# A ternary product fed by two float32r parts of its rows instead of three bfloat16 parts, in a one-core perceiver kernel

## The chip, the cores and the metric

The kernel runs on one core of one Trainium2 chip. The core has five engines with queues of their own: TensorE (PE; its weight loads are listed as PEld), VectorE (DVE), ScalarE (ACT), GpSimd (POOL) and SyncE (SP), which here only issues transfers. The metric is the device time of one execution in microseconds; the figure for a kernel is the median of its runs.

## What is computed

The reference is a two-layer perceiver over 128 independent batches of 32 latent rows (width 256) and 257 context rows each. Cut to its last lines it is

```python
x = x + _L0_xattn_ref(ctx_1024, _layernorm(x), wq, wk, wv)     # softmax attention over the context
x = x + _L0_attn_ref(_layernorm(x), ...)                        # selective scan, 512 channels x 16 states
x = x + _L0_ffn_ref(_layernorm(x), W_fc, ln_w, ln_b, W_proj)    # the feed-forward that the change touches
x = x + _L1_xattn_ref(_layernorm(x), ctx_1024, ctx_1024, ...)   # linear attention with focused feature maps
x = x + _L1_attn_ref(_layernorm(x), ...)                        # latent attention with decay
x = x + _L1_ffn_ref(_layernorm(x), w1, b1, w2, b2)              # quantized feed-forward
```

and the part that matters is

```python
def _L0_ffn_ref(x, W_fc, ln_w, ln_b, W_proj):
    h = jnp.einsum('btd,hd->bth', x, absmean(W_fc))     # absmean: every weight becomes -1, 0 or 1
    h = jax.nn.gelu(h, approximate=False)
    h = layernorm(h, ln_w, ln_b)
    return jnp.einsum('bth,dh->btd', h, absmean(W_proj))
```

The first product has 256 inputs and 1024 hidden units. Its weights are ternary, so they are exact in any type; the precision of the product is that of the rows `x`.

## The kernel before

**Tiling.** Four batches of 32 rows make a group of 128 rows, which fill the 128 partitions; there are 32 groups. Groups are taken in nine blocks of 2, 4, 4, 4, 4, 4, 4, 4 and 2 (`BLOCKS`). For each block the program records, one after the other: for each group the context part (`context_group`: loads, transposes of the context, softmax attention, then keys and values for the linear attention of layer 1, in the tiles `pkey`, `ku`, `ks`, `pval`, `vf` and `pk`); the scan of the whole block (`scan_block`: projections `pproj`, then for each of 4 x 16 channel-state pairs an exponential `a` on ACT, a scan `h` on DVE and a weighted sum on DVE or POOL); and for each group the latent part (`latent_group`: `mlp`, `linear`, `attention`, `quantized_mlp`).

**What sets the order.** Nothing is issued as it is recorded. A `Recorder` collects all operations with their reads, writes and an estimated duration, and `order` (L403) places them like a list scheduler. Every recorded part has a window in the table `DUE`, from which each operation gets a due time; on each engine the operation due soonest goes first among those that could start soon enough (`WINDOW`). `SOONER` favours operations that free PSUM, `AHEAD` pulls transfers forward, `HORIZON` limits how far ahead a new buffer is opened. An operation that may run on several engines (`copy`: ACT or DVE; `cast`: ACT or POOL) goes where its start, plus its duration weighted by `PRICE`, is lowest. The order that comes out is a fixed program order on each engine, and each engine works strictly along it. All these operations are issued from one line, L575, in `trace`; names of tiles tell them apart.

**Buffers.** Tiles come from rings: `t4` (4 buffers of 4 KB per partition), `t2` (17 of 2 KB, `t2k`, L693), `t1` (7 of 1 KB, `t1k`) and eight PSUM banks (`bank`). The plan may open a tile only where the ring has a buffer free. The 2 KB ring serves, among others, the scan's `h`, `dl`, `some` and four `yg` a block, `ku` and `ks` of the keys, and `x3` below.

**Fill products.** Where the plan leaves PE idle for more than 600 ns, `keep_busy` (L553) adds products of constants into the bank that is about to be used, issued from L562:

```python
for _ in range(int(FILL * (op.gap - 200.0) / 216.0)):      # FILL is 0.7
```

They compute nothing that is used.

**The first product of the MLP** (`mlp`, L1223). The rows of a group, less their mean, are transposed by PE into a bank `pT` and copied by ACT to `xT` (f32). Then they are split into three bfloat16 parts in the tile `x3` (the profile shows it as `x`): a cast, a subtraction on POOL of what the cast kept, a second cast, and a second subtraction on POOL that writes the third part. For each half of the 1024 hidden units, six products accumulate in one bank `ph`: two halves of the 256 inputs times three parts, each 128 x 128 x 512 in bfloat16, with the rows as stationary operand and `w_fc` as moving one. ACT applies the gelu, DVE takes statistics, PE transposes `hid`, and the second product `pmlp` runs in plain f32. `w_fc` is made once, in `late_setup`, by the function `ternary`, which writes -1, 0 and 1 straight into a bfloat16 tile (L746) of 4 KB per partition.

**Key-value sums** (`keys_values`, L1121). Each group adds four sums, one a batch, into the bank `pk`; the last one recorded closes the accumulation.

Of the kernel before, what the change touches and what calls it, by code (L numbers as in the profile page):

```python
# [9 lines left out]
BF16 = mybir.dt.bfloat16  # L10
I32 = mybir.dt.int32
AF = mybir.ActivationFunctionType
ALU = mybir.AluOpType
# [3 lines left out]
P = 128  # L17
# [91 lines left out]
def size_of(a):  # L109
    n = 1  # L110
    for k in a.shape[1:]:
        n *= k
    return n
# [153 lines left out]
class Recorder:  # L267
# [62 lines left out]
    def record(self, calls):  # L330
        ways = {}
        for engine, (name, args, kw) in calls.items():
# [25 lines left out]
            ways[engine] = [(name, args, kw)], ns, locks  # L358
        reads = [b for b in map(box_of, ins) if b]
        writes = [b for b in map(box_of, outs) if b]  # L360
        bufs = [a.buf for a in (*ins, *outs) if isinstance(a, View)]
        self.keep += bufs
        self.bufs_of.update((id(b), b) for b in bufs)
        if self.joined is not None:
            small = ins[0].shape[0] < P or size_of(ins[0]) < P
            self.joined.append((*ways["tensor"][:2], reads, writes, small))
            return
        landing = 0
        if "sync" in ways:
            size = size_of(out) * P * 4 if writes else 0  # L370
            landing = 2000 + size / 180.0
        self.add(ways, reads, writes, table, landing)
# [218 lines left out]
PRICE = {"tensor": 0.0, "vector": 28.013093, "scalar": 4.356996, "gpsimd": 3.720234, "sync": 0.0}  # L591
WINDOW = 13.821085
SOONER = 0.0675
AHEAD = 0.744939
HORIZON = 1.665209
# [3 lines left out]
def perceiver_kernel(ctx: ExitStack, tc: tile.TileContext, t: dict, out: bass.AP):  # L599
# [93 lines left out]
    def t2k(shape, name, dtype=F32):  # L693
        return ring("t2", 17).tile(shape, name, dtype)

    def t1k(shape, name, dtype=F32):
        return ring("t1", 7).tile(shape, name, dtype)
# [48 lines left out]
    w_fc = wts.tile([P, 2, HID], BF16, name="w_fc")  # L746
# [246 lines left out]
    def context_group(b0, xg, kvc):  # L993
# [91 lines left out]
        with R.together():  # L1085
            for m in range(8):
                t_ = slice(m % 4 * 32, m % 4 * 32 + 32)
                R.tensor.matmul(
                    pk[t_, m // 4].rearrange("p b k -> p (b k)"),
                    plg[:, m * 32 : (m + 1) * 32],  # L1090
                    vlz[:, m].rearrange("p b k -> p (b k)"),
                    start=m < 4, stop=False,
                )
        for b in range(0, GB, PAIR):
            zs = keys(cTs[b : b + PAIR])
            for i in range(PAIR):
                keys_values(cTs[b + i], zs[i], pk[:, :, b + i, :], b + i == GB - 1)
# [23 lines left out]
    def keys_values(cT, z, pk, last):  # L1121
# [20 lines left out]
        R.gpsimd.tensor_copy(vf[:, :, :, 16], f.unsqueeze(2).to_broadcast([P, 2, NH]))  # L1142
        with R.together():
            for c in range(2):
                for j in range(2):
                    for m in range(4 * c, 4 * c + 4):
# [5 lines left out]
                        )  # L1152

# [69 lines left out]
    def mlp(xg):  # L1223
# [3 lines left out]
        xT = t1k([P, D], "xT")  # L1227
        transposed(xc, xT.rearrange("p (c n) -> p c n", c=2), 2)

        x3 = t2k([P, 3, D], "x3", BF16)  # L1230
        R.cast(x3[:, 0, :], xT)
        R.gpsimd.tensor_tensor(xT, xT, x3[:, 0, :], ALU.subtract)
        R.cast(x3[:, 1, :], xT)
        R.gpsimd.tensor_tensor(x3[:, 2, :], xT, x3[:, 1, :], ALU.subtract)
# [3 lines left out]
        for k in range(2):  # L1238
            ph = bank("ph")
            cols = slice(k * 512, (k + 1) * 512)  # L1240
            with R.together():
                accumulate(ph, [
                    (x3[:, k3, dc * P : (dc + 1) * P], w_fc[:, dc, cols])
                    for dc in range(2) for k3 in range(3)
                ])
# [267 lines left out]
    (-1.233024, -0.335498), (0.019828, 0.480193), (-1.629912, -0.869437), (-0.837897, -0.738361),  # L1513
    (-0.093681, -0.088914), (-0.021839, -0.017211), (0.306149, 0.488484), (0.39917, 0.543159),
    (0.505346, 1.339487), (0.48714, 0.600075), (0.577018, 0.904067), (0.865508, 1.005891),
    (1.046044, 1.425814), (1.390255, 1.643429), (1.317874, 1.43935), (1.798509, 1.951231),
    (2.102721, 2.277249), (2.253363, 2.602763), (2.83034, 2.835295), (1.877067, 1.881711),
    (1.451009, 1.899495), (0.786758, 1.881711), (1.887508, 2.002024), (0.636118, 0.718999),
    (0.728345, 0.76535), (0.753626, 0.774222), (0.721695, 1.041519), (1.02934, 1.176199),
    (1.193086, 1.242338), (1.482066, 1.506436), (1.570038, 1.574756), (1.52572, 1.568128),  # L1520
    (1.582666, 1.870871), (1.996577, 2.069774), (2.143081, 2.422113), (2.358304, 2.65149),
    (2.69793, 2.755759), (2.394754, 2.76594), (2.909432, 3.128141), (3.227729, 3.512565),
    (3.409932, 3.76627), (2.727973, 3.098836), (3.085723, 3.337484), (3.365331, 3.681179),
    (3.656735, 4.119898), (2.875393, 3.198347), (3.111345, 3.33781), (3.418247, 3.706203),
    (3.705912, 4.06225), (3.050509, 3.381501), (3.357332, 3.56083), (3.584301, 3.855628),
    (3.839172, 4.228837), (1.635373, 1.790687), (1.595887, 1.641535), (1.962785, 2.117782),
    (2.053357, 2.161526), (2.195383, 2.199528), (2.205476, 2.209605), (2.389908, 2.395792),
    (2.486901, 2.49243), (2.488439, 2.647508), (2.615044, 2.87897), (2.840922, 3.128108),
    (3.030885, 3.414002), (3.317041, 3.762668), (3.556818, 3.693699), (3.66408, 3.911331),
    (3.779069, 4.169666), (4.40464, 4.40964), (4.420203, 4.76275), (3.72375, 4.048085),  # L1530
    (4.091394, 4.323445), (4.208163, 4.522378), (4.569256, 4.925594), (3.85714, 4.180094),
    (4.257484, 4.482106), (4.435791, 4.690815), (4.424337, 4.851387), (3.983018, 4.55219),
    (4.391584, 4.396584), (4.348461, 4.54678), (4.768461, 5.107725), (2.594693, 2.67371),
    (2.676285, 2.763798), (2.912055, 2.916796), (2.949665, 3.029696), (3.19548, 3.202614),
    (3.201985, 3.267525), (3.370849, 3.437113), (3.357869, 3.499671), (3.422175, 3.546126),
    (3.536298, 3.791633), (3.827101, 4.085596), (4.097429, 4.412778), (4.392392, 4.655498),
    (4.693, 4.866463), (4.036996, 4.310319), (4.858234, 5.11216), (5.047385, 5.382144),
    (5.400897, 5.766052), (4.741086, 5.03528), (5.046704, 5.271326), (5.279494, 5.56433),
    (5.556414, 5.882502), (4.706208, 4.941658), (5.205771, 5.425698), (5.421318, 5.709504),
    (5.507902, 5.512902), (5.023502, 5.345889), (5.321575, 5.568746), (5.570116, 5.854452),  # L1540
    (5.880912, 6.216796), (3.643344, 3.71582), (3.765067, 3.84418), (3.787796, 3.900941),
    (4.065296, 4.070275), (4.162677, 4.239555), (4.077256, 4.22408), (4.388544, 4.42773),
    (4.425818, 4.457414), (4.539487, 4.592008), (4.671053, 4.971619), (4.919167, 5.210754),
    (5.182193, 5.441083), (5.441083, 5.698089), (5.733278, 5.738278), (5.27428, 5.53055),
    (5.897482, 6.1173), (5.879768, 6.449337), (6.407415, 6.764085), (5.692519, 6.052832),
    (6.046377, 6.27138), (5.860084, 6.537213), (6.550022, 6.906966), (5.877385, 6.208316),
    (6.196681, 6.421303), (6.422896, 6.706139), (6.695526, 7.043141), (6.036972, 6.355891),
    (6.270476, 6.526377), (6.57082, 6.856055), (6.792378, 7.195162), (4.655912, 4.660912),
    (4.67689, 4.774904), (4.974338, 4.979338), (5.031969, 5.241355), (5.15376, 5.208739),
    (5.208182, 5.362023), (5.36406, 5.420469), (5.452575, 5.58779), (5.498786, 5.63902),  # L1550
    (5.613721, 5.894373), (5.872873, 6.132026), (6.156801, 6.412601), (6.400357, 6.652506),
    (6.652075, 6.657075), (6.553174, 7.05071), (6.816602, 6.998958), (7.18521, 7.372307),
    (7.415066, 7.753978), (6.720233, 7.046956), (7.022044, 7.269572), (7.354633, 7.359633),
    (7.519057, 7.88096), (6.879083, 7.195618), (7.19559, 7.440215), (7.420282, 7.694224),
    (7.705356, 8.061949), (7.020903, 7.344351), (7.361654, 7.570043), (7.532526, 7.817798),
    (7.900297, 8.217473), (5.571057, 5.60675), (5.694226, 5.774033), (5.850032, 5.910131),
    (5.899092, 5.961479), (6.160411, 6.165411), (6.187877, 6.292569), (6.437907, 6.442483),
    (6.440971, 6.515481), (6.499997, 6.614903), (6.615753, 6.87484), (6.873594, 7.132682),
    (7.131911, 7.39192), (7.391788, 7.650876), (7.652298, 7.698741), (7.687389, 7.904001),
    (7.908329, 8.089699), (7.975111, 8.03271), (8.430878, 8.761522), (7.723787, 7.798595),  # L1560
    (8.152372, 8.33892), (8.301126, 8.415202), (9.120664, 9.680432), (8.269822, 8.363895),
# [92 lines left out]
```

## Time and profile before

| | |
|---|---|
| time, median of 3 runs | 1715.9 us (1712.74, 1715.9, 1718.06) |
| span of the profiled execution, first to last instruction | 1714.2 us (a time of its own is not listed for it; the median lies 1.7 us above its span) |
| PE, PEld busy | 1650.3 us, 1200.9 us |
| DVE, ACT, POOL busy | 1501.8, 1422.8, 1362.6 us |
| chain that ended last, by engine | PE 48%, DVE 24%, ACT 15%, POOL 10% |
| products into `ph` | 384, 91.5 us |
| granted TensorE clock, mean | 0.996 |

The profile was taken by the hardware profiler on one execution. The page gives busy time, share and count for each engine, and then the span in 40 equal slices, in which a digit is the busy share in tenths. In the table of groups a line reads: line, engine, operation, output <- inputs with their shapes, count; then busy time and mean ns of one; then the idle time of that engine just before, and what ended it. Several products in flight overlap, so the busy time of a group is less than count times mean. A product in plain f32 shows as two records. "The chain" follows the last instruction back, step by step, to what released it.

### The profile page before, as it was taken

The page shows a single profiled execution, that of the slowest core. Times are in us where ns is not written, and L with a number is a line of the kernel's source. Part 1 is how long each engine was busy: PE and PEld are TensorE (multiplying, and loading weights), DVE is VectorE, ACT ScalarE, POOL GpSimd, SP SyncE. Part 2 cuts the span into 40 slices and gives each one's busy share as a digit, 9 for nine tenths or more (in the row PEclk, how much of TensorE's full clock was granted, in tenths as well). Part 3 has the DMA queues.
Part 4 walks back from the last instruction along what each step waited for, and adds up shares of the span by engine and source line. Part 5 has one row for each costly group of instructions (what it writes and reads, how often), then busy time and mean ns, then how long its engine had stood idle before and what let it go on. Part 6 is the DMA issues. An engine that isn't in the chain of part 4 may idle for free.

```text
span 1714.2 us, 45797 instructions
## 1 busy us (share of the span) xinstructions
PE 1650.3 (96%) x17587; PEld 1200.9 (70%) x17587; DVE 1501.8 (88%) x2960; ACT 1422.8 (83%) x3484; POOL 1362.6 (79%) x2152
## 2 busy tenths in 40 slices
PE   8999999999999999999999999999999989899986
PEld 6778777767677767766777777777777666666664
DVE  5389699988997997959998997979999899999777
ACT  4587789888988899779888998889998888788676
POOL 6668769768795888688878678886898699788887
PEclk9999999999999999999999999999999999999999
DMA  8312100110010102001100012010110000000000
GB/s 235 99 60 72 30 29 30 57 35 7 29 54 5 35 14 63 30 2 45 38 30 29 8 42 63 3 29 10 61 42 30 2 20 8 4 4 2 5 9 22
DMA packets 44762, 59.74 MB, mean 35 GB/s; under 512 B 8704, under 2 KB 27008, under 8 KB 44544
## 3 DMA queue, kind: packets, MB, share of 16 engines
q1 hardware_dynamic: 44544, 56.81, 10.7%
q8 instruction: 139, 2.28, 0.6%
q14 instruction: 79, 0.65, 0.1%
HBM read 52.32 MB, written 4.19 MB: 33 GB/s over the span
## 4 chain that ended last, share of the span: by engine, by line
PE 48%; DVE 24%; ACT 15%; POOL 10%; issue 3%; DMA 0%; DVEq 0%; POOLq 0%; ACTq 0%; SPq 0%
DVE h L575 10%; PE pkey L575 7%; PE pproj L575 7%; PE pval L575 6%; DVE acc L575 5%; PE pT L575 3%; PE pmlp L575 3%; PE pqa L575 3%; POOL ku L575 3%; ACT a L575 2%; PE pk L575 2%; ACT ks L575 2%; ACT L575 2%; PE pka L575 2%; PE pcT L575 2%
## 5 line engine op out<-in xcount | busy, mean ns | idle before, releaser
L575 DVE TENSOR_TENSOR_SCAN h<-a,pproj 128x512 f32<-128x512 f32 (+1 forms) x576 | 613.9, 1087 | 22.6 <-ACT a L575 12.5
L575 ACT ACTIVATE a<-dl,a_neg 128x496 f32<-128x496 f32 (+1 forms) x576 | 367.5, 664 | 57.7 <-DVE h L575 53.6
L575 DVE SCALAR_TENSOR_TENSOR acc<-h,w_st,acc 128x512 f32<-128x512 f32 (+1 forms) x436 | 299.9, 688 | 0.7
L575 PE MATMUL pval<-wkv,cT 128*128 128x256 f32 x1024 | 243.9, 384 | 0.1
L575 PE MATMUL pkey<-wkv,cT 128*128 128x256 f32 x1024 | 238.1, 386 | 0.0
L575 ACT ACTIVATE ks<-ku 128x256 f32<-128x256 f32 x512 | 209.1, 415 | 19.3 <-POOL ku L575 17.9
L575 PEld LDWEIGHTS pkey<-wkv,cT 128*128 128x128 f32 x1024 | 189.3, 190 | 39.0 <-issue 15.6
L575 PEld LDWEIGHTS pval<-wkv,cT 128*128 128x128 f32 x1024 | 188.0, 190 | 32.0 <-issue 4.5
L575 POOL TENSOR_TENSOR ku<-ku,e 128x512 f32<-128x512 f32 x128 | 162.8, 1280 | 31.3 <-ACT ku L575 30.0
L575 POOL TENSOR_TENSOR ku<-ks,ku 128x512 f32<-128x512 f32 x128 | 164.4, 1290 | 16.9 <-ACT ks L575 15.8
L575 POOL TENSOR_TENSOR kn<-kn,halves 128x4 f32<-128x4 f32 x128 | 134.3, 1052 | 23.5 <-ACT ks L575 21.9
L575 ACT ACTIVATE vf<-pval,kf 128x256 f32<-128x256 f32 x256 | 108.3, 475 | 31.1 <-PE pval L575 26.3
L575 POOL TENSOR_TENSOR rstd<-rstd,halves 128x1 f32<-128x1 f32 x224 | 126.1, 567 | 6.1
L575 PE MATMUL pproj<-xTs,w_in 128*128 128x512 f32 (+1 forms) x288 | 122.8, 554 | 2.2 <-DVE x L575 1.3
L575 ACT ACT_TABLE_LOAD x95 | 121.9, 1283 | 2.3 <-DVE hq L575 0.6
L575 POOL TENSOR_TENSOR some<-some,h 128x512 f32<-128x512 f32 (+1 forms) x104 | 115.2, 1107 | 3.5
L575 PE MATMUL pmlp<-w_pr,hT 128*128 128x256 f32 x512 | 117.3, 383 | 0.6 <-DVE x L575 0.6
L575 PEld LDWEIGHTS pmlp<-w_pr,hT 128*128 128x128 f32 x512 | 96.2, 191 | 14.7 <-DVE x L575 0.7
L575 POOL TENSOR_SCALAR h<-h,w_st 128x512 f32<-128x512 f32 (+1 forms) x104 | 65.3, 629 | 51.0 <-DVE h L575 32.7
L575 ACT ACTIVATION_READ_ACCUMULATOR ks<-ku 128x1 f32 x512 | 100.8, 197 | 0.0
L575 POOL TENSOR_SCALAR rstd<-mv 128x1 f32<-128x1 f32 x224 | 45.4, 203 | 67.5 <-DVE mv L575 43.3
L575 PE MATMUL ph<-w_fc,x 128*128 128x512 bf16 x384 | 91.5, 380 | 0.3 <-ACT vf L575 0.2
(289 smaller groups left out, 3867.0 us busy)
## 6 DMA issues: line engine op xcount, KB each, us to landing
cx<-in_ctx_dram SPq DMA_DIRECT2D x64, 512.0 KB
x<-in_x_dram SPq DMA_DIRECT2D x32, 128.0 KB
cr<-in_ctx_dram SPq DMA_DIRECT2D x128, 32.0 KB
out_dram<-x SPq DMA_DIRECT2D x32, 128.0 KB
vlz<-vl SPq DMA_DIRECT2D x128, 1.1 KB
w_in<-in_w_inT_dram SPq DMA_DIRECT2D x1, 1024.0 KB
raw_fc<-in_w_fcT_dram SPq DMA_DIRECT2D x2, 512.0 KB
raw_pr<-in_w_prT_dram SPq DMA_DIRECT2D x2, 512.0 KB
```

What stands on the lines that cost most here:

```text
L575: ins = getattr(engine, name)(*(traced(a) for a in args), **{k: traced(v) for k, v in kw.items()}).ins
```

## The change

- `w_fc` becomes a tile of type float32r, with four bytes an element, so 8 KB per partition in place of 4.
- `mlp` keeps the transposed rows in the bank `pT` and makes two float32r parts of them, in two 1 KB tiles (both named `xT` and a number): a copy of the bank, on ACT or DVE, and on DVE the bank less that copy. The f32 copy `xT`, the tile `x3`, both casts and both subtractions on POOL go.
- A half of the hidden units is now four products (two halves of the inputs times two parts) in place of six.
- The 2 KB ring has 15 buffers in place of 17.
- `PRICE`, `WINDOW`, `SOONER`, `AHEAD`, `HORIZON` and the whole table `DUE` have new values, so every engine's order is new.
- The recorder's `record` is split in two (`cost` is new) and takes lists of calls; no call hands it one. `keys_values` takes the list of the sums placed before it, and the last sum of a group must follow the other three.

```diff
-PRICE = {"tensor": 0.0, "vector": 28.013093, "scalar": 4.356996, "gpsimd": 3.720234, "sync": 0.0}
-WINDOW = 13.821085
-SOONER = 0.0675
-AHEAD = 0.744939
-HORIZON = 1.665209
+PRICE = {"tensor": 0.0, "vector": 45.207809, "scalar": 8.002797, "gpsimd": 6.895979, "sync": 0.0}
+WINDOW = 13.504066
+SOONER = 0.067879
+AHEAD = 0.971922
+HORIZON = 1.829143
...
-        return ring("t2", 17).tile(shape, name, dtype)
+        return ring("t2", 15).tile(shape, name, dtype)
...
-    w_fc = wts.tile([P, 2, HID], BF16, name="w_fc")
+    w_fc = wts.tile([P, 2, HID], F32R, name="w_fc")
...
+        last = len(sums) == GB - 1
+        R.first = tuple(sums) if last else ()
         with R.together():
...
-        xT = t1k([P, D], "xT")
-        transposed(xc, xT.rearrange("p (c n) -> p c n", c=2), 2)
-
-        x3 = t2k([P, 3, D], "x3", BF16)
-        R.cast(x3[:, 0, :], xT)
-        R.gpsimd.tensor_tensor(xT, xT, x3[:, 0, :], ALU.subtract)
-        R.cast(x3[:, 1, :], xT)
-        R.gpsimd.tensor_tensor(x3[:, 2, :], xT, x3[:, 1, :], ALU.subtract)
+        xs = [t1k([P, D], f"xT{k}", F32R) for k in range(2)]
+        pt = bank("pT")
+        with R.together():
+            for c in range(2):
+                cols = slice(c * P, (c + 1) * P)
+                R.tensor.transpose(pt[:, cols], xc[:, cols], ident)
+        R.copy(xs[0], pt[:, 0:D])
+        R.vector.tensor_tensor(xs[1], pt[:, 0:D], xs[0], ALU.subtract)
...
                 accumulate(ph, [
-                    (x3[:, k3, dc * P : (dc + 1) * P], w_fc[:, dc, cols])
-                    for dc in range(2) for k3 in range(3)
+                    (part[:, dc * P : (dc + 1) * P], w_fc[:, dc, cols])
+                    for dc in range(2) for part in xs
                 ])
```

## The prediction, made before the changed kernel ran

> **What bounds the kernel now.** I read the page's busy shares and slices first.
>
> ```profile
> span 1714.2 us, 45797 instructions
> PE 1650.3 (96%) x17587; PEld 1200.9 (70%) x17587; DVE 1501.8 (88%) x2960; ACT 1422.8 (83%) x3484; POOL 1362.6 (79%) x2152
> ...
> PE   8999999999999999999999999999999989899986
> DVE  5389699988997997959998997979999899999777
> ```
>
> PE is busy everywhere, and DVE is close behind. A share for the whole span mixes three stages, so I asked next for the busy time of each engine by stage (columns: window, its length, then busy us and instructions of PE, PEld, DVE, ACT, POOL, then clock, DMA share, GB/s).
>
> ```profile
> 0.00:100.00 100.00, 94.83 (x854) 70.92 (x855) 52.00 (x125) 53.39 (x168) 63.82 (x113) 1.00 0.52 156
> 100.00:1300.00 1200.00, 1186.69 (x12689) 872.00 (x12687) 1083.98 (x2031) 1042.74 (x2608) 953.13 (x1483) 1.00 0.11 33
> 1300.00:1430.00 130.00, 122.72 (x1267) 86.61 (x1267) 122.74 (x212) 111.65 (x249) 108.49 (x163) 1.00 0.06 19
> 1430.00:1714.00 284.00, 246.08 (x2786) 171.37 (x2784) 243.09 (x596) 215.06 (x463) 237.15 (x396) 0.97 0.02 7
> ```
>
> From 100 to 1300 us PE stands still for only 13.3 us of 1200: there the time is PE's work, and what PE loses in work the kernel can lose in time. After 1300 PE stands still for 7.3 + 37.9 = 45.2 us; there chains through all engines set the pace. The same table for the fill products (line 562, which the kernel inserts where its plan leaves PE idle) has 58 of them before 100 us, none from 100 to 1300, and 110 after, 1.56 + 30.45 = 32.0 us busy.
>
> Then the groups of PE by shape, and its weight loads.
>
> ```profile
> L575 PE MATMUL pproj<-xTs,w_in 128*128 128x512 f32 x224 | 106.2, 601 | 2.2 <-DVE x L575 1.3 <-ACT vf L575 0.9
> L575 PE MATMUL ph<-w_fc,x 128*128 128x512 bf16 x384 | 91.5, 380 | 0.3 <-ACT vf L575 0.2
> ...
> L575 PEld LDWEIGHTS pmlp<-w_pr,hT 128*128 128x128 f32 x512 | 96.2, 191 | 14.7 <-DVE x L575 0.7 <-issue 0.4 <-ACT ks L575 0.2
> ...
> L575 PEld LDWEIGHTS <-x 128*128 128x128 bf16 x384 | 36.4, 98 | 40.7 <-issue 3.8 <-POOL x L575 0.6 <-ACT xT L575 0.2
> ```
>
> The mean of one product (380 ns) overlaps its neighbours; busy time over count is what one costs: 91.5 / 384 = 238 ns for ph, and 106.2 / 224 = 474 ns for one record of a plain f32 product of 512 columns, of which each such product has two. Hardly anything is waited for ahead of ph (0.3 us).
>
> Last, the operations on the tile xT, which prepare the rows (min/median/max ns), and the DVE group that is most like the new subtraction.
>
> ```profile
> L575 ACT CAST x<-xT x39: 389/405/440, 381.7 to 1613.1; 128x256 bf16<-128x256 f32 x39
> L575 POOL TENSOR_TENSOR xT<-xT,x x32: 668/672/682, 231.4 to 1612.4; 128x256 f32<-128x256 f32 x32
> L575 POOL TENSOR_TENSOR x<-xT,x x32: 668/674/778, 233.3 to 1615.5; 128x256 bf16<-128x256 f32 x32
> L575 POOL CAST x<-xT x25: 395/398/420, 229.9 to 1445.9; 128x256 bf16<-128x256 f32 x25
> ```
>
> ```profile
> L575 DVE TENSOR_TENSOR y<-pn,y 128x256 f32<-128x256 f32 x32 | 13.1, 409 | 2.0 <-POOL y L575 1.8
> ```
>
> **The products.** Each of the 32 groups goes from 12 products of 128x512 to 8, so 384 become 256. The trace has no float32r product. Its nearest rows are bf16 at 512 columns (238 ns; 216 where twelve stand back to back, 2.59 us on the chain) and one record of f32 at 512 columns (474 ns). The lower end is 216: no 512-column row is below it. I take 238, because of the ratio of the rows: a plain f32 product is 2 x 474 = 948 ns, 3.98 times the bf16 one, which reads as two pieces of each operand, four passes at the bf16 pace; a part that TensorE takes whole then needs one. The ternary weights lose nothing by it, and the second part carries what the first leaves. So 128 fewer at 238 ns: 30.5 us less PE work. With 216 for the new ones it is 36.2 less; with 474 it is 121.3 - 91.5 = 29.8 more. By the table of ph by stage (264 records from 100 to 1300, 24 up to 1430), 22 groups lie in the PE-bound stage: 22 x 0.95 = 21.0 us of the 30.5; the other 9.5 lie where PE also has gaps.
>
> **The weight loads.** The new stationary operand has four bytes: by the rows a load is 190 ns instead of 98. On the chain 16 records of pmlp, with loads of 191, take 3.46 us, 216 each: loads lie under products. Only the first load of each half of the hidden layer can show, 64 x 92 ns = 5.9 us as the upper end; I take nothing, since PE's loader pulls it under the product before.
>
> The Trainium skill's page "TensorE: Matmul & The Clock Gate", Part 3, The mechanism, states that a weight load overlaps with a running matmul only where their row groups differ. That speaks against this change: full 128-row loads would then add, 12 x (98 + 216) = 3.77 us a group before and 8 x (190 + 216) = 3.25 after, and the saving would be 16.6 us in place of 30.5. The 3.46 us for 16 records contradict it.
>
> **The fills and the plan.** The changed program's order holds 204 fill products instead of 168: 57 in the setup, 16 in nine places of what was the gapless middle, and 131 (for 110) in the last part, spread over 43 places for 33. A fill stands where the plan has PE idle for over 600 ns, so the new plan returns part of the gain as gaps: two buffers fewer of 2 KB, and a search that ended elsewhere. What a fill stands for I bound by rows: its own 32.0 / 110 = 0.29 us, and with all idle time after 1300 us charged to it, (45.2 + 32.0) / 110 = 0.70. In the setup it is (5.2 + 16.7) / 58 = 0.38. I take 0.5, between them: 36 x 0.5 = 18.0 us back (10.4 to 25.2). I charge the smaller ring of buffers here and not again.
>
> **The rows' preparation.** ACT loses 39 casts (15.5 us) and by the order 4 of 96 table loads (4 x 1.283 = 5.1), POOL loses 25 casts and 64 subtractions (9.9 + 21.5 + 21.7 = 53.1). None of it is on PE, so in the PE-bound stage it is worth nothing. As latency, copy, cast, subtraction, cast, subtraction (0.37 + 0.41 + 0.67 + 0.40 + 0.67 = 2.5 us) become copy and subtraction (0.78). In the last block ph follows directly on phq in PE's queue, so I take nothing; the lower end is two groups in turn, 3.5 us, and the table loads' 5.1.
>
> DVE gains 32 subtractions with one operand in PSUM. I take 409 ns, the same operation on the same shape and memories: 13.1 us (8.9 by the 278 ns of the 128x128 row, 15.3 by the 478 ns of the costliest row of this width). In the middle DVE has 1200 - 1084 = 116 us idle and gets 22 x 0.41 = 9.0 of it, so it is covered; with no cover left the whole 13.1 comes back. All 32 first copies stay on ACT, and no other operation changes engine. Keeping pT until DVE has read it holds one of eight banks about 0.4 us longer: nothing.
>
> **What has one answer.** w_fc is written as 4 bytes: its two ternary operations took 1283 ns each to bf16, and w_pr's of the same size 1284 to f32, so nothing. The added order among the four key-value sums concerns only the last sum of each group, whose operands come last anyway: nothing. SP's queue is reordered (loads asked for earlier); one context load stands on the chain for 5.20 us at 1230, so that is worth between -5.2 and +5.2, taken as 0.
>
> **Sum.** -30.5 + 18.0 = -12.5 us. The profiled span of 1714.2 becomes 1701.7; the median of the runs lies 1.7 above that span, so 1703.4 us. With the fills' bounds alone it is 1696 to 1711.
>
> **The rivals.** *PE waits for DVE.* The second product of each ph now waits for DVE's subtraction, where it waited for POOL; DVE works in order and is 90% busy in the middle (POOL 79%), so the subtraction can stand behind a scan of 1.2 us. Behind the waiting product stand all of PE's keys, values and projections, and behind these ACT and POOL. PE's similar waits today cost 10.2 us in 11 times (pqT for POOL's q), 0.93 each. At that price for all 32 groups: 29.8 - 12.5 = +17.3, 1733 us. It decides from a mean wait of 12.5 / 32 = 0.39 us. For it: DVE's load. Against: ph's own wait for two operations of POOL is next to nothing today. 0.18.
>
> *Float32r at two passes.* 474 ns a product: 29.8 + 18.0 = +47.8, 1764 us; the edit would then not do what it says. Every record in the trace whose operands have 4 bytes is of the slower kind, which speaks for it; the ratio of four against. 0.07.
>
> *Nothing left.* The plan's gaps are dearer than 0.70 and DVE, now 13 us fuller, becomes the pace in the middle: 1711 to 1721, taken at 1716. 0.13.
>
> *All of it.* Fills hide in idle time that is there anyway, and the shorter chain and fewer table loads count in the last part: -30.5 - 3.5 = -34, 1682 us; a half of it 1690. 0.12.
>
> The forecast itself keeps 0.50. What this kernel's measurement can tell from no change is about 0.3%, 5.1 us. Faster by more: 0.50 + 0.12 = 0.62, less 0.02 for the forecast's own upper edge; within: 0.13 + 0.02; slower: 0.18 + 0.07. The range runs from 1688, inside the best case, to 1728, inside the first rival, whose wait may be smaller than 0.93; that leaves out the two passes, part of the first rival and the end of the best case.
>
> **What would show it.** In the changed profile: 256 records of ph near 61 us busy; ph's idle time still under 2 us, the releaser not DVE; PE idle in the middle about 13 us plus some 4; a subtraction near 409 ns x32; POOL about 53 us lower. I am wrong if ph costs 474 ns, or shows 512 records, or if PE's waits for DVE in the middle add up to more than 12 us.

## The result, and the profile after

The changed kernel takes 1722.85 us (median of 7 runs, 1720.31 to 1725.65), the kernel before 1717.28 (median of 7 beside them). The ratio is 1.0037, 95% interval 1.0025 to 1.0049: it is slower, by 6.4 us. The forecast was 1703.4.

The profiled execution lasted 1718.6 us from first to last instruction (its own time is 1720.31, the lowest of the seven). Its page, the busy line, two rows of slices and the chain's shares:

```profile
span 1718.6 us, 45554 instructions
...
PE 1636.2 (95%) x17465; PEld 1209.2 (70%) x17495; DVE 1513.6 (88%) x2992; ACT 1406.5 (82%) x3441; POOL 1311.0 (76%) x2063
...
PE   9999999999999999999999999999999988888897
...
DVE  5499599989997799969999998989999899999787
...
PE 41%; DVE 25%; ACT 16%; POOL 13%; issue 5%; DVEq 0%; POOLq 0%; ACTq 0%
```

PE, ACT and POOL are busy for less time than before (-14.1, -16.3, -51.6 us), DVE for 11.8 us more, and the end comes later. PE's part of the chain fell from 48% to 41%; DVE and ACT gained a point each and POOL three. Busy time by stage, in the columns used for the kernel before:

```profile
0.00:100.00 100.00, 95.57 (x864) 70.81 (x865) 50.40 (x131) 52.83 (x168) 62.95 (x115) 1.00 0.54 168
100.00:1300.00 1200.00, 1174.29 (x12547) 877.89 (x12566) 1092.70 (x2043) 1034.28 (x2582) 915.93 (x1412) 1.00 0.10 32
1300.00:1430.00 130.00, 118.98 (x1267) 83.85 (x1268) 117.87 (x208) 106.88 (x236) 99.40 (x151) 1.00 0.06 19
1430.00:1718.00 288.00, 247.35 (x2794) 176.68 (x2799) 252.61 (x613) 212.54 (x458) 232.67 (x388) 0.99 0.02 7
```

From 100 to 1300 us PE now stands still for 25.7 us, where it was 13.3. (This trace lacks 30 records of one group, `phq`, 19 of them here: 12547 against 12566 weight loads. At 0.24 us each the idle time is some 4.6 us too long.) The groups that the prediction spoke of, of PE, of PE's loader and of DVE:

```profile
L587 PE MATMUL ph<-w_fc,xT 128*128 128x512 f32 x256 | 76.8, 426 | 2.4 <-DVE xT L587 2.0
...
L587 PEld LDWEIGHTS ph<-w_fc,xT 128*128 128x128 f32 x256 | 45.3, 189 | 15.8 <-DVE xT L587 3.2 <-issue 2.4 <-ACT ku L587 0.9
...
L587 DVE TENSOR_TENSOR xT<-pT,xT 128x256 fp32r<-128x256 f32 x32 | 13.0, 406 | 2.9 <-POOL x L587 2.8
```

Busy time over count, the measure that the prediction used, is 76.8 / 256 = 300 ns, not 238. This measure counts overlap with the neighbours: the first product of each half begins 29 ns after its predecessor here, and 215 ns after it in the kernel before (medians of 64). From start to start, the later products of a half come every 232 ns here and every 216 before. By these PE is relieved of 384 x 0.216 - 256 x 0.232 = 23.6 us, not of 30.5; its busy time falls by less because it has 36 fill products more (56.5 us for 48.7). The subtraction takes 406 ns (forecast 409), and PE waits for it once, 2.0 us. Fill products stand 57 before 100 us, 16 in the middle and 131 after, as the program orders them.

### The profile page after: what moved, and what is told of

It reads as the page before. It is cut to its first block, busy times and chain, and to the rows that moved or that the text cites. A ratio compares the mean times of both kernels' runs of the same rounds, so it can differ in the third digit from the quotient of the medians.

```text
span 1718.6 us, 45554 instructions
## 1 busy us (share of the span) xinstructions
PE 1636.2 (95%) x17465; PEld 1209.2 (70%) x17495; DVE 1513.6 (88%) x2992; ACT 1406.5 (82%) x3441; POOL 1311.0 (76%) x2063
## 4 chain that ended last, share of the span: by engine, by line
PE 41%; DVE 25%; ACT 16%; POOL 13%; issue 5%; DVEq 0%; POOLq 0%; ACTq 0%
DVE h L587 10%; PE pkey L587 7%; DVE acc L587 7%; PE pval L587 6%; PE pproj L587 5%; POOL ku L587 3%; ACT a L587 3%; PE pT L587 3%; PE pmlp L587 2%; ACT L587 2%; POOL some L587 2%; PE pk L587 2%; ACT ks L587 2%; PE pqa L587 2%; POOL rstd L587 1%
## 5 line engine op out<-in xcount | busy, mean ns | idle before, releaser
L587 ACT ACTIVATE ks<-ku 128x256 f32<-128x256 f32 x512 | 209.2, 414 | 13.6 <-POOL ku L587 10.2
L587 POOL TENSOR_TENSOR ku<-ks,ku 128x512 f32<-128x512 f32 x128 | 163.2, 1283 | 20.5 <-ACT ks L587 18.9
L587 ACT ACTIVATE ku<-pkey 128x512 f32<-128x512 f32 x128 | 73.0, 592 | 14.8 <-PE pkey L587 11.7
```

What stands on the lines that cost most here:

```text
L587: ins = getattr(engine, name)(*(traced(a) for a in args), **{k: traced(v) for k, v in kw.items()}).ins
```

## The experiments

All ratios are to the kernel before, run beside it on the same chip, with 95% intervals. "+8 us" is the difference of ratios times 1717. "The old order" is the program order of the kernel before, "the new order" that of the changed one; in most experiments the order is kept and only what is issued at one step is changed.

### Is it the price of float32r?

**Two bfloat16 parts in the new order.** The changed kernel with bfloat16 parts and weights; nothing else moves.

```diff
-    w_fc = wts.tile([P, 2, HID], F32R, name="w_fc")
+    w_fc = wts.tile([P, 2, HID], BF16, name="w_fc")
...
-        xs = [t1k([P, D], f"xT{k}", F32R) for k in range(2)]
+        xs = [t1k([P, D], f"xT{k}", BF16) for k in range(2)]
```

> The changed kernel with its two parts and the weights in bfloat16 instead of float32r; every engine's order is the same, and the product is less exact. Theory A (a float32r product costs 300 ns where I took 238, and that is paid on the path): 256 x 62 ns = 15.9 us less PE work, 22 of 32 groups in the stretch where PE sets the pace, so 11 to 16 us under the changed kernel: 1707 to 1712 us. Theory B (the new order loses the time, the product's price lies beside idle time): within 3 us of the changed kernel's 1722.9.

Measured: 1724.42 us, 1.0041 [1.0028, 1.0054], the same as the changed kernel (the two intervals leave some 3 us). The dearer product costs nothing that can be told.

**A series of products behind the end.** After the last instruction of the changed kernel PE runs 24 products each of: bfloat16; float32r with 128, 64 and 32 stationary columns; float32r over 256 moving columns; float32r with one stationary tile throughout; plain f32; bfloat16 over 256 columns.

```diff
+    series(tc, ps, R, w_fc, w1, w_pr)
...
+        for i in range(24):
+            ins = nc.tensor.matmul(d, left, right, start=True, stop=True).ins
```

> The changed kernel with eight series of 24 products behind its last one, whose results nobody uses: bfloat16 and float32r at 512 columns, float32r with 64 and 32 instead of 128 stationary columns, float32r and bfloat16 at 256 columns, float32r with the same stationary tile each time, plain f32. If a float32r product is paced by its weight load (189 ns for 128 columns), the 64-column series falls to the bfloat16 pace of 216 ns and the 256-column series stays near 190 to 260; if the moving operand's four bytes slow it, 64 columns change nothing and 256 columns halve it to about 130 ns.

PE's timeline (start, length, group; the first three float32r series come as one, x72, and one bfloat16 record is missing of 24):

```profile
1721.72 5.34 PE L621 MATMUL s_bf<-w 128*128 128x512 bf16 x23
1726.71 16.88 PE L621 MATMUL s_r<-w_fc 128*128 128x512 f32 x72
1743.43 3.04 PE L621 MATMUL s_r128n<-w_fc 128*128 128x256 f32 x24
1746.32 5.62 PE L621 MATMUL s_r<-w_fc 128*128 128x512 f32 x24
1751.78 20.76 PE L621 MATMUL s_f<-w_pr 128*128 128x512 f32 x48
1772.38 2.78 PE L621 MATMUL s_bf16n<-w 128*128 128x256 bf16 x24
```

With the last product's own length (0.38 us) taken off, bfloat16 comes every (5.34 - 0.38) / 23 = 216 ns and float32r every (16.88 - 0.39) / 71 = 232 ns; plain f32 every 20.76 / 48 = 433 ns a record, two to a product. So float32r is one pass, 7% slower than bfloat16. Its pace hardly changes with loads of 188, 134 and 109 ns (128, 64 and 32 columns: 235, 230 and 232 ns) and with one stationary tile (227), so the loads do not set it. Of the two accounts that I had written down, a pace set by the load is refuted. The signs of the other came (64 columns change nothing, 256 columns take half, 120 ns), but what it has to explain is 16 ns a product, not the 62 that I had read from busy time.

### Does PE's work set the time?

**Eight of twelve products in the old order.** The third parts are left out of the sum, and all else of the kernel before is issued as it was.

```diff
+            if op.engine == "tensor" and calls[0][1][0].buf.name == "ph":
+                calls = [c for i, c in enumerate(calls) if i % 3 < 2]
+                calls[-1] = (*calls[-1][:2], {"start": False, "stop": True})
```

> The kernel before, in its own order, with the products of the third bfloat16 part left out (8 of 12 a group; the third part is still made but not used). Theory A (PE sets the pace from 100 to 1300 us): 128 products of 238 ns less, 20.9 us in that stretch and up to 9.5 after it: 1687 to 1696 us. Theory B (DVE, 90% busy there, takes over as soon as PE gets faster): at most 5 us faster, 1712 or more.

Measured: 1715.1 us, 0.9989 [0.9979, 0.9999]. The relief is 28 us (91.5 less the 63.5 us that 256 such products cost in the complete trace of a run with the same order; 128 at 216 ns are 27.6); the time falls by 1.9. PE's waits of this run from 100 to 1300 us (waited for: total, times, longest) say where it went:

```profile
PE pk L579 <- POOL vf L579: 3.2, 7, 0.8
PE pT L579 <- ACT hid L579: 3.2, 2, 2.2
PE pqT L579 <- POOL q L579: 3.0, 5, 0.8
PE poq L579 <- ACT qT L579: 2.8, 4, 1.2
```

In the kernel before, these took 0.4, 0.3, 0.9 and 1.0 us in the same stage. PE arrives earlier and waits for POOL and ACT, at several places, a little at each. The granted TensorE clock is a little lower too: 0.989 to 0.995 on average in these executions, 0.992 to 0.998 in those of the kernel before. At 0.995 alone it is 1712.1 to 1712.7 us against 1716.0 to 1716.7 of the kernel before in all its runs, so the relief is worth 3 to 5 us there, still far from 28.

**Twelve bfloat16 products in the new order.** The two-part bfloat16 kernel with the second of each pair issued twice.

```diff
+                calls = [calls[i] for i in (0, 1, 1, 2, 3, 3)]
```

> The changed kernel's order with bfloat16 parts and twelve products a group again (the second part is multiplied twice, so the result differs): as much PE work as before, in the new order and with the new preparation. Theory A: 128 x 238 ns = 30.5 us of work more than with eight, of which 21 to 30 us show, so 1730 to 1740 us; what it stands above the kernel before (13 to 23 us) is the price of the new order. Theory B (PE is not the pace in the new order): under 10 us above the same with eight.

Measured: 1729.82 us, 1.0080 [1.0066, 1.0094], 6.7 us above the eight products. Of some 28 us added to PE (128 products at 216 ns) 6.7 show in the new order.

**Sixteen products in the old order**, the mirror image of eight.

```diff
+                calls = [calls[i] for i in (0, 1, 2, 2, 3, 4, 5, 5)]
```

> The kernel before in its own order with 16 products a group instead of 12 (the third part is multiplied twice): 128 more at 238 ns, 30.5 us more PE work. Theory E (PE tight): 20 to 28 us slower, 1737 to 1745. Theory F: under 12 us slower, as the new order was with 128 products more.

Measured: 1732.34 us, 1.0089 [1.0076, 1.0102]: `ph` costs 120.1 us for 91.5, and of these 28.6 us more 15.3 show, between the two outcomes that I had expected. The middle of this run:

```profile
100.00:1300.00 1200.00, 1190.67 (x12615) 873.52 (x12614) 1077.24 (x2009) 1035.05 (x2586) 945.48 (x1470) 1.00 0.11 33
```

PE's idle time, 13.3 us before, is 9.3: hardly any was there to take the added work. Four products more a group cost 15.3 us, four fewer bring 1.9.

### What does the subtraction on DVE cost?

**No subtraction.** The changed kernel without the second part; the first part is multiplied twice, so PE does the same.

```diff
+            if op.engine == "vector" and isinstance(out, View) and out.buf.name == "xT1":
+                continue
+            if op.engine == "tensor" and out.buf.name == "ph":
+                calls = [(n, a, k) for i in (0, 2) for n, a, k in (calls[i], calls[i])]
```

> The changed kernel in its own order, with the 32 DVE subtractions not issued and the first part multiplied twice: DVE work as in the kernel before, PE work as in the changed kernel. Theory B (the added DVE work is what the changed kernel pays): about as fast as with one part and four products, 1716 to 1719. Theory D (in the new order PE's work counts too): 1720 or more.

Measured: 1714.68 us, 0.9990 [0.9980, 1.0001], 8.1 us below the changed kernel for 13.0 us of DVE's work. (Without the subtraction the bank `pT` also comes free earlier; in the changed kernel's trace only the load of one fill product, which reads constants, waits for the subtraction, 1.1 us.)

**One part: no subtraction, four products.**

```diff
+            if op.engine == "vector" and isinstance(out, View) and out.buf.name == "xT1":
+                continue
+            if op.engine == "tensor" and out.buf.name == "ph":
+                calls = calls[0::2]
```

> The changed kernel in its own order without the second part: the 32 DVE subtractions are not issued, and four products a group are, of the first part only (less exact). DVE is back at the work of the kernel before, PE has 31 us less than the changed kernel. Theory B: the 13 us of DVE come back, 1707 to 1712. Theory C: the new order stays as slow as it is, 1718 or more.

Measured: 1717.07 us, 0.9994 [0.9984, 1.0003], between the two that I had expected. PE has 128 products less than in the last run, and the time is no lower.

**The subtraction kept, four products** (the second half of the last edit alone).

> The changed kernel in its own order with the subtractions, and with four products of the first part a group in place of eight: 31 us less PE work, everything else as in the changed kernel. Theory B: within 2 us of the changed kernel, 1721 to 1725. Theory D: 4 to 7 us faster, 1716 to 1719.

Measured: 1725.18 us, 1.0048 [1.0036, 1.0061]. `ph` costs 46.9 us here instead of 76.8, and the time is that of the changed kernel. Against one part without the subtraction it is 9.3 us more. With PE full or relieved, and whether or not a product reads its result, the subtraction costs 8 to 9 us.

**The same work added to DVE in the old order**: the product `oa` (410 ns) issued twice in each group.

```diff
+            if op.engine == "vector" and isinstance(out, View) and out.buf.name == "oa":
+                calls = calls * 2
```

> The kernel before, with one DVE operation of the latent attention (oa from poa and sm, 128x256, one operand in PSUM, 410 ns) issued twice in each of the 32 groups: the same DVE work that the change adds, 13.1 us, with everything else and every order as before. Theory B (DVE sets the pace): 8 to 13 us slower than before, 1726 to 1731. Theory C (no engine's total counts, the new order of the work loses the time): within 3 us of before.

Measured: 1721.52 us, 1.0028 [1.0017, 1.0039]: +4.8 us for 13.6 (`oa` 26.7 us busy for 13.1), between the two that I had expected. This adds work to DVE and nothing else, so DVE's time alone costs something; that it is less than the subtraction's cost may lie in the other place or the other order.

**The old order with one part**: the kernel before with four products, and without the second cast and both subtractions on POOL.

```diff
+                if name_ == "x3" or (name_ == "xT" and calls[0][1][2].buf.name == "x3"):
+                    continue
...
+            if op.engine == "tensor" and name_ == "ph":
+                calls = calls[0::3]
```

> The kernel before in its own order with one bfloat16 part: the second cast and both POOL subtractions are not issued, four products a group are. PE has 61 us less work than the kernel before, POOL 48, ACT 9, DVE the same: nearly the work of the changed kernel with one part, in the old order. Theory C (the new order is worse by itself): 1705 to 1711, 6 to 12 us under the same work in the new order. Theory B: the two orders are equal, 1714 to 1718.

Measured: 1717.75 us, 1.0008 [0.9997, 1.0018]. With one part in both, the old order (17 buffers of 2 KB) and the new one (15) take the same time to within 2.4 us. The old one had a lower granted clock in these runs (0.985 to 0.990, the new one 0.992 to 0.997), so at an equal clock it would be ahead; by how much, no run shows.

**The second part on POOL.** The changed kernel in float16: the copy of the bank goes to an f32 tile, POOL casts it and subtracts.

```diff
-    w_fc = wts.tile([P, 2, HID], F32R, name="w_fc")
+    w_fc = wts.tile([P, 2, HID], F16, name="w_fc")
...
+                for m, b in (
+                    ("tensor_copy", (two[:, 0, :], whole)),
+                    ("tensor_tensor", (two[:, 1, :], whole, two[:, 0, :], ALU.subtract)),
+                ):
+                    ins = getattr(self.nc.gpsimd, m)(*b).ins
```

> The changed kernel in its own order with the second part made on POOL: ACT copies the transposed rows to SBUF in f32, and at the place of DVE's subtraction POOL casts the first part (0.40 us) and subtracts (0.67 us); parts and weights in float16, as exact in the weights and near 22 bits in the rows. DVE has 13 us less than the changed kernel, POOL 34 more. Theory B (the DVE work is what the change pays): 1714 to 1718, as without the subtraction. If a later second part or POOL's work costs as much: 1720 or more.

Measured: 1733.95 us, 1.0097 [1.0084, 1.0110], 18.4 us above the run without a subtraction. POOL's two groups of this run, and PE's wait for them:

```profile
L602 POOL TENSOR_TENSOR xT<-xT,xT 128x256 f16<-128x256 f32 x32 | 21.5, 672 | 2.6
L602 POOL CAST xT<-xT 128x256 f16<-128x256 f32 x32 | 12.8, 401 | 5.7 <-ACT xT L619 5.6
```

```profile
PE ph L619 <- POOL xT L602: 6.4, 13, 1.5
```

They add 34.3 us to POOL, which is the least busy of the four engines (78% in this run), and over half of that shows, in all more than on DVE. PE waits for them 13 times, 0.5 us each; the rest of the 18.4 us I could not place.

### Is another engine the pace?

Each of these takes work off one engine of the kernel before, in the old order: on **DVE** the largest absolute value of the hidden row `hq` over 256 of its 1024 columns (-25.5 us), on **POOL** no addition of `s0` (-24.3), on **ACT** the sum of squares `junk` over 256 columns (33.8 to 13.3, -20.5).

```diff
+            if op.engine == "vector" and calls[0][0] == "tensor_reduce" and name_ == "amax2":
+                calls = [(n, (a[0], a[1][:, 0:256], *a[2:]), k)]
...
+            if op.engine == "gpsimd" and calls[0][0] == "tensor_tensor" and calls[0][1][2] is s0_of[0]:
+                continue
...
+            if op.engine == "scalar" and name_ == "junk":
+                calls = [(n, (a[0][:, 0:256], a[1][:, 0:256], *a[2:]), k)]
```

> The kernel before with the largest absolute value of the second feed-forward's hidden row taken over 256 of its 1024 columns: 32 DVE operations of 1.21 us become 0.41 us, 25.7 us less DVE work; orders unchanged. Theory B: 15 to 25 us faster, 1693 to 1703. Theory C: at most 5 us faster.

Measured for DVE: 1715.61 us, 0.9983 [0.9973, 0.9993], -2.9.

> The kernel before without the addition of s0 to the rows, 32 POOL operations of 761 ns, 24.3 us less POOL work (the result lacks that term); orders unchanged. Theory B: within 4 us of before, POOL is 79% busy. If POOL's chains set the pace instead: 12 us faster or more.

Measured for POOL: 1717.8 us, 0.9993 [0.9982, 1.0004], -1.2, no change that can be told.

> The kernel before in its own order with the squares of the second feed-forward over 256 of 1024 columns: 32 ACT operations of 1.06 us become about 0.3 us, some 24 us less ACT work. Theory F (chains of the order; each relief alone shows little): 0 to 5 us faster, 1712 to 1717. If ACT is the engine that sets the pace: 15 us or more.

Measured for ACT: 1713.91 us, 0.9981 [0.9972, 0.9990], -3.3.

**PE and DVE relieved together** (eight products and the shorter maximum).

> The kernel before in its own order with both reliefs at once: eight of twelve products a group (PE 30 us less) and the absolute maximum over 256 of 1024 columns (DVE 25.7 us less). Alone they gave about 2 and 3 us. Theory E (PE and DVE are both tight in the middle, so each holds the time when the other is relieved): 10 to 20 us faster than before, 1697 to 1707. Theory F (neither's total sets the pace; the order's chains do): the sum of the two, 1711 to 1713.

Measured: 1710.97 us, 0.9966 [0.9954, 0.9978], -5.8; the two singles add to -4.8.

**All four relieved together.**

> The same, and also POOL without the addition of s0 (24.3 us less) and ACT with the squares of the second feed-forward over 256 of 1024 columns (about 25 us less). Theory E with more than two tight engines: 15 to 25 us faster, 1692 to 1702. Theory F: 1706 to 1712.

Measured: 1705.23 us, 0.9933 [0.9921, 0.9945], -11.5; the four singles add to -9.3. Nearly 100 us of work less on four engines brings 11.5; the reliefs about add up, and none unlocks another. The middle of this run, whose trace lacks no matmul:

```profile
100.00:1300.00 1200.00, 1173.39 (x12697) 866.42 (x12697) 1075.06 (x2037) 1035.38 (x2616) 942.09 (x1466) 1.00 0.11 33
```

PE stands still for 26.6 us, twice as long as in the kernel before, and every other engine has gaps of over 100 us.

### What do the two missing buffers cost?

**Seventeen buffers under the new order.** The two-part bfloat16 kernel, whose `w_fc` leaves room for them; the plan is still made for 15, but the 2 KB ring has 17.

```diff
-                self.shape, self.dtype, tag=self.ring.tag, name=self.name, bufs=self.ring.n
+                self.shape, self.dtype, tag=self.ring.tag, name=self.name, bufs=self.ring.n + 2 * (self.ring.tag == "t2")
```

> The changed kernel's order with bfloat16 parts and weights (which leave the space) and 17 real buffers of 2 KB where the order was planned for 15: no engine waits for one of the two buffers. If the smaller ring costs time in the run itself: 3 us or more under the same with 15, 1721 or less. If it acts only through the plan: 1722 to 1726.

Measured: 1715.39 us, 0.9993 [0.9983, 1.0002], 8.2 us below the same kernel with 15 (1.0041). DVE's scans in both, first with 15 buffers, then with 17:

```profile
L587 DVE TENSOR_TENSOR_SCAN h<-a,pproj 128x512 f32<-128x512 f32 x448 | 533.0, 1206 | 20.2 <-ACT a L587 10.4 <-POOL some L587 8.7 <-POOL ku L587 0.2
```

```profile
L587 DVE TENSOR_TENSOR_SCAN h<-a,pproj 128x512 f32<-128x512 f32 x448 | 532.6, 1206 | 10.5 <-ACT a L587 9.8 <-POOL ku L587 0.2
```

With 15 the scan waits 8.7 us for POOL's weighted sum `some`. The scan reads nothing of `some`; what it waits for is the buffer, still read by POOL, that the next `h` is to be written to. With 17 that releaser is gone and nothing takes its place, and the saving in time is of the same size. Counted from the first scan (97.3 and 95.9 us), the 449th, with which the eighth block begins, starts 2.9 us earlier with 17 (1352.8 and 1348.5), the last 8.2 us earlier (1610.9 and 1601.3). These are one execution each, the second the fastest of its eleven, at a clock of 0.999 against 0.996.

This is what two buffers more than planned bring, and not yet what the change lost. The kernel before has its 17 buffers planned for as well, with `x3` among the tiles that take them, and its scan waits for `some` just as long. DVE's wait in the kernel before, then in the changed one (total, times, longest):

```profile
DVE h L575 <- POOL some L575: 8.4, 9, 2.3
```

```profile
DVE h L587 <- POOL some L587: 8.9, 11, 1.5
```

The run without a subtraction has this wait too, 8.2 us with 15 buffers, and is as fast as the kernel before. Two buffers above the plan of the old order were not tried.

### A version that beats both

**Two float16 parts in the old order.** The kernel before with `x3` and `w_fc` in float16, 17 buffers, one cast, one subtraction on POOL (which was there already) and eight products; DVE has nothing new to do.

```diff
-    w_fc = wts.tile([P, 2, HID], BF16, name="w_fc")
+    w_fc = wts.tile([P, 2, HID], F16, name="w_fc")
...
-        x3 = t2k([P, 3, D], "x3", BF16)
+        x3 = t2k([P, 3, D], "x3", F16)
...
+                if name_ == "x3":
+                    continue
...
+                calls = [c for i, c in enumerate(calls) if i % 3 < 2]
```

> The kernel before in its own order with two float16 parts: first cast, one POOL subtraction that writes the second part, eight products; the second cast and second subtraction are not issued, weights in float16, 17 buffers. PE has 30 us less work than before, POOL 26, ACT 9, DVE the same. By the small effect that each engine's relief had alone (3 us for PE, 1 for POOL): 1712 to 1716; if reliefs of several engines help each other: 1705 to 1711.

Measured: 1713.97 us, 0.9985 [0.9976, 0.9995]. It beats both kernels, the one before by 2.6 us only: the order is still the one planned for twelve products. A plan searched anew for it was not tried.

## Why the prediction was wrong

Inside the range, on the wrong side. Its steps in turn:

**What bounds the kernel** is the step that failed: "From 100 to 1300 us PE stands still for only 13.3 us of 1200: there the time is PE's work, and what PE loses in work the kernel can lose in time." The first half is right and the second does not follow. A relief of PE alone of nearly that size, with the order and the buffers untouched, brought 1.9 us of 28. PE's small idle time says that work *added* to PE shows (15.3 of 28.6 us), not that work taken away does. Each engine runs a fixed order; when PE arrives earlier it waits a little for POOL at one place, for ACT at the next. Four reliefs of 20 to 28 us brought between 1.2 and 3.3 us each, and together about their sum: no one engine is the pace, and PE and DVE are not the pace together. That fits chains that pass through all four; which chains, no run isolates.

**The products.** One pass, as the ratio of the rows had it; the size was off by a quarter. The reading "busy time over count is what one costs" does not hold: the last product of a run, 379 ns long, overlaps with the group behind it. Bfloat16 in runs of four shows 64.9 / 256 = 254 ns (the kernel with 17 buffers), in runs of six 238, and from start to start 216 in both:

```profile
L587 PE MATMUL ph<-w_fc,xT 128*128 128x512 bf16 x256 | 64.9, 379 | 3.0 <-DVE xT L587 2.4 <-ACT ku L587 0.4 <-ACT hid L587 0.2
```

With 216 and 232 the term is 23.6 us in place of 30.5. It does not decide, as the bfloat16 kernel took the same time.

**The weight loads** hide, as taken. By the rule of the Trainium skill's page "TensorE: Matmul & The Clock Gate", Part 3, The mechanism, that a load overlaps with a running matmul only where their row groups differ, my estimate from the rows is 190 + 216 = 406 ns a product. The kernel shows 232 from start to start, and so does the series, with loads of 188.

**The fills** came as counted, 36 more, but they were charged as time given back by the plan, 18.0 us with the smaller ring inside. Like the 30.5 us this priced PE's time as the kernel's. With all of the new order's fills the bfloat16 kernel with 17 buffers stands at 0.9993, and the kernel without a subtraction, with 15, at 0.9990. So new plan and smaller ring together cost a few us at most as the times stand, not 18. What the ring alone costs against the kernel before, no run shows.

**The rows' preparation.** POOL lost 51.6 us and ACT 16.3, worth little, as said (reliefs of 24.3 and 20.5 us brought 1.2 and 3.3). The second failure is DVE: 13.1 us "so it is covered", taken as zero, cost 8.1 to 9.3. The 116 us of idle time in the middle were no full cover. The subtraction's duration is as forecast, and PE hardly waits for it (2.0 us, once), so the cost lies elsewhere, most likely in DVE's own queue behind it, and it comes mostly late: against the run without it (one execution each), the 449th scan starts 0.9 us later (1352.7 and 1351.7), the last 3.6 us later (1609.3 and 1605.7) and the end comes 5.6 later (spans 1718.6 and 1713.0); its first scan starts 0.9 us earlier (96.5 and 97.4). The text had the whole 13.1 as the case without cover; I took zero because I looked at the middle alone, and ten of the 32 subtractions lie after it.

**The sum.** With the measured terms it is about -2 for PE and +8 for DVE, so +6; measured +6.4. The 8.2 us of the two buffers are no third term, as the wait that they take away stood in the kernel before too. The agreement is partly luck, because the granted clock differs and the prediction did not think of it: in the last stage it is 0.97 before and 0.99 after, as the two tables show. Run beside the experiments, the kernel before took 1712.9 to 1714.1 us where its mean clock was 0.998 and 1714.2 to 1716.6 at 0.996; the changed kernel took 1720.7 at 0.998 and 1722.9 to 1725.7 at 0.996. At an equal clock the change costs nearer 8 us, and some us of the new order are not accounted for. Why the new order keeps more of the clock, no run shows.

Two buffers more, or no subtraction, each alone bring the time back to that of the kernel before. The changed kernel with both at once was not tried.

**The rivals.** *PE waits for DVE* ended on the right side by the wrong road: the waits of PE for DVE in the middle add to 8.7 us (3.7 before), below the 12 that I named. *Two passes* is refuted by the series. *Nothing left* was nearest in its cause, "DVE, now 13 us fuller, becomes the pace", though it still counted on PE's relief, and 1722.85 lies past its end. *All of it* would have needed PE on the path; half of its -34 would be 1699, not 1690.

**The signs.** Three failed: `ph` 76.8 us busy (61 named), its idle time 2.4 us with DVE as releaser (under 2, not DVE), PE idle for 25.7 us in the middle (17). The subtraction's time and POOL's relief came. Of the three things that were to show me wrong (474 ns a product, 512 records, 12 us of waits for DVE) none came: they watch the terms, and none asks whether the time follows PE's work.

**Open.** Which chain the second part on POOL lengthens by so much (10.3 us above the changed kernel), how much a plan made for 17 buffers would gain, and what two buffers above its plan would bring the old order.

## What to carry to other kernels

A high busy share warned of what added work costs here (15.3 of 28.6 us) and did not tell what removed work brings (1.9 of 28): before a relief is counted, leave the work out in the same order and look whether the time follows, or the engine's idle time. Where several engines run fixed orders and wait for each other, work added to the second fullest can show by a third to three quarters of its size, whatever idle time its row has. The worth of a ring's buffers shows in the waits of the operation that writes into it; two more than planned brought 8.2 us here. Before such a gain is called the cost of a change, look whether the same wait stood in the kernel before.

## What the runs showed of the hardware

A float32r product of 128x512 comes every 232 ns in a long run (bfloat16 216, a record of plain f32 433), whatever its number of stationary columns. Of 256 columns it takes about 120 ns, bfloat16 109 ((3.04 - 0.28) / 23 and (2.78 - 0.27) / 23, the last product's own length taken off). ACT's copy from a bank into float32r takes 372 ns and DVE's subtraction out of a bank 406, as long as their f32 kin:

```profile
L587 ACT COPY xT<-pT x96: 348/372/438, 10.8 to 1674.0; 128x256 f32<-128x256 f32 x96
L587 ACT CAST xT<-pT x32: 349/372/419, 215.8 to 1620.9; 128x256 fp32r<-128x256 f32 x32
```
